# A two-level Strassen kernel in fp32: block 0's second load in two parts, weight loads held back, and six more products split a third time

## The chip, the core and the metric

The kernel runs on one core of one Trainium2 chip. The time is device microseconds of one execution. The engines named below are PE (TensorE, matrix products), DVE (VectorE), ACT (ScalarE), POOL (GpSimd, which here also issues the gathers) and SP (SyncE, which issues the other transfers).

## What is computed

The input x is 64 sequences of 64 tokens, 1024 features each, in fp32. Two steps are added to it:

```
x = x + A0[id0] . (B0[id0] . x)             # per sequence: an adapter of rank 16
base   = W x                                 # 1024 x 1024
logits = Wr x + 5 * onehot(id1)              # 8 experts, the best two get softmax weights
lora   = sum over experts of gate_e * B1_e (A1_e x)
x = x + base + 2 * lora
```

The kernel keeps tokens along the free axis, so x is 1024 x 4096 (features x tokens) and almost all the work is W x.

## The kernel before

The 4096 tokens are 8 blocks of 512. Two blocks make a pair, and there are four pairs, `s` = 0 to 3. For each block, `early` does the first adapter: `turn` transposes the gathered rows of B0 (tile `gb`) on PE into `pt`, ACT copies them to `bt`; `project` multiplies them with x into `pb`, DVE masks that into `bx`; `adapt` multiplies `bx` with the gathered rows of A0 (tile `ga`) into four `px` tiles for each half of the features, and DVE adds these to x. `late` does the router: `rows` gives `ph`, `gates` the expert weights on DVE, `weigh` transposes them through `pg` into `hg`.

`products` computes W x for a pair as 2 x 2 blocks with the Strassen-Winograd scheme, twice nested. The seven outer products have the numbers n in `ORDER = (1, 2, 6, 7, 5, 3, 4)`. Each of them has seven inner products k of a 256 x 256 weight tile (`s` tiles, 256 KB) with 256 x 256 tokens: four fp32 matmuls of 128 x 128 weights on 256 columns, in PSUM tiles `pa` and `pb`. Pair 0 makes the sums of weights that the scheme needs and writes them to `s_kept` in DRAM; later pairs load them. Inner products of some n can be split a third time ("fine"): seven matmuls on 128 columns in place of four on 256, in a tile `pf`, in four parts that the order puts between other products. A fine product needs sums of weights (`sf`, four operations of POOL or DVE, kept in DRAM as `f_kept` and loaded later), sums of tokens (`tt`, three operations), three ACT copies into `cp`, and two DVE additions of 128 x 256. `fine_of(s, n)` says which k are split: none in pair 0, k = 2 and 4 in the later pairs, only k = 2 in the last product of the last pair.

Nothing is ordered by hand. Every step is handed to a `Plan` with the engines that can do it and its estimated cost, what it reads and writes, the slot it takes, and a due time `at`. `Plan.order` (L64) simulates the engines with these estimates and fixes each engine's instruction order; the program then waits on semaphores only. `behind` makes a step be issued only after another one has been issued. A `hold` is a POOL copy of one column into a tile that is about to be loaded: the load has to wait for it, and it waits for the data that it reads. In the kernel before:

- `load(0, 0)` loads the first half of block 0 (features 0 to 511) in two transfers of 512 KB; `load(0, 1)` loads the second half in one of 1 MB, held until the first of these two has landed.
- `load_w` loads the sixteen 256 KB tiles of W, each behind the load of A1 (`a_sb`), which is itself held until block 0's `gb` has landed.
- `b1_sb` is loaded behind A1.
- PSUM slots are eight: four of tag `l` (`pt`, `pb` of `project`, `px`, `ph`, `pg`, part of `pf`), two `a`, two `b`.
- In `products`, pairs with `s < FINE` take one branch for the order of the steps (L1222 to L1232), the others the branch for fine products.

Of the kernel before, what the change touches and what calls it, by code (L numbers as in the profile page):

```python
# [14 lines left out]
P = 128  # L15
# [159 lines left out]
def kernel(  # L175
# [52 lines left out]
    TB = 512  # L228
    NBLK = NT // TB
    NSUP = NBLK // 2  # L230
# [16 lines left out]
    WHOLE = {(0, 1)}  # L247

    FINE = 1
    FOURTH = (1, 2, 6, 7, 5, 3, 4)  # L250
    THIRD = ()

    pe, dve = Pinned(tc, nc.tensor), Pinned(tc, nc.vector)
    act, pool, sp = Pinned(tc, nc.scalar), Pinned(tc, nc.gpsimd), Pinned(tc, nc.sync)
# [14 lines left out]
    def new(tag, shape, name):  # L269
        return pools[tag].tile(shape, F32, tag=tag, name=name)  # L270
# [38 lines left out]
    def consts():  # L309
        plan.add({"SP": 0.4}, lambda e: sp.dma_start(wr_c, wr), [], [("wr_c",)], -53, kb=8)  # L310
        plan.add(
            {"SP": 0.4}, lambda e: sp.dma_start(ids1_sb, ids1[0:1, :].to_broadcast([P, NB])),
            [], [("ids1",)], -53, kb=32,
        )

        def hold(e):

            pool.tensor_copy(a1_sb[:, 0, :1], made["gb", 0][:, :1])

        plan.add({"POOL": 0.2}, hold, [(("gb", 0),)], [("a1",)], -56)  # L320
        plan.add({"SP": 0.4}, lambda e: sp.dma_start(a1_sb[:, :, :P], a1), [], [("a1",)], -45, kb=512)
        plan.add({"SP": 0.4}, lambda e: sp.dma_start(b1_sb, b1), [], [("b1",)], -29, kb=512, behind=[("a1",)])

        def spread(e):
            pool.tensor_copy(a1_sb[:, :, P:], wr_c)

        plan.add({"POOL": 0.3}, spread, [("wr_c",)], [("wr",)], -45)
# [26 lines left out]
    def part(t, cs=range(HC), gs=range(NG)):  # L354
        return [(t, c, g) for c in cs for g in gs]
# [7 lines left out]
    def load(k, i, at):  # L363
        t = ("x", k, i)

        held = (k, i) == (0, 1)

        def hold(e):

            made[t] = new("q", [P, HC, TB], f"x_{k}_{i}")  # L370
            pool.tensor_copy(made[t][:, 0, :1], made["x", 0, 0][:, 0, :1])


        cuts = ((0, HC // 2), (HC // 2, HC)) if (k, i) == (0, 0) else ((0, HC),)

        def fn(c0, c1):
            if not held and c0 == 0:
                made[t] = new("q", [P, HC, TB], f"x_{k}_{i}")
            sp.dma_start(
                made[t][:, c0:c1],  # L380
                xT[(i * HC + c0) * P : (i * HC + c1) * P, k * TB : (k + 1) * TB].rearrange(
                    "(c p) t -> p c t", p=P
                ),
            )

        if held:
            plan.add(
                {"POOL": 0.2}, hold, part(("x", 0, 0), [0]), part(t), at, [("q", t)]
            )
        for c0, c1 in cuts:  # L390
            plan.add(
                {"SP": 0.5}, lambda e, c0=c0, c1=c1: fn(c0, c1),
                [], part(t, range(c0, c1)), at, [("q", t)] * (not held and c0 == 0),
                kb=256 * (c1 - c0), behind=[("a1",)] * (k == 1) + [(t, 0, 0)] * (c0 > 0),
            )
# [249 lines left out]

    def load_w(i, j, at):
        t = w_name[i, j]

        def fn(e):
            made[t] = new("s", [P, QC, QO], f"w_{i}{j}")  # L650
            sp.dma_start(made[t], w[:, j * QC : (j + 1) * QC, i * QO : (i + 1) * QO])

        plan.add({"SP": 0.4}, fn, [], [(t,)], at, [("s", t)], kb=256, behind=[("a1",)])

    def add_identity(i, at):

# [18 lines left out]
    def fine_of(s, n):  # L675

        if s < FINE:
            return ()
        if (s, n) == (NSUP - 1, ORDER[-1]):
            return (2,)  # L680
        return (2,) + (4,) * (n in FOURTH) + (3,) * (n in THIRD)


    def combine(out, a, b, op, at, engines):
# [33 lines left out]
    def weights(s, n, at):  # L718

        out = {}  # L720
        if s > 0:
            for i, m in enumerate(ORDER):
                out[m] = t = ("s", s, n, m)

                def fn(e, t=t, m=m):
                    made[t] = new("s", [P, QC, QO], f"s_{s}_{n}{m}")
                    sp.dma_start(made[t].rearrange("p c o -> p (c o)"), s_kept[n - 1, m - 1])

                plan.add({"SP": 0.1}, fn, [("kept", n, m)], [(t,)], at + i - 8, [("s", t)], kb=256)
            wt[n] = out  # L730
            for k in fine_of(s, n):
                fine_weights(s, n, k, out[k], at + (k == 4) * 5)
            return
        m = m_q[n]
        out = {1: m[0, 0], 2: m[0, 1], 4: m[1, 1]}
        for k, (u, v, op) in {
            5: ((1, 0), (1, 1), ALU.add),
            6: (5, (0, 0), ALU.subtract),
            7: ((0, 0), (1, 0), ALU.subtract),
            3: ((0, 1), 6, ALU.subtract),  # L740
        }.items():
            out[k] = ("s", s, n, k)
            uu = m[u] if isinstance(u, tuple) else out[u]
            vv = m[v] if isinstance(v, tuple) else out[v]
            combine(out[k], uu, vv, op, at - 4, {"DVE": 0.65})
        for k in ORDER:
            t = out[k]

            def keep(e, t=t, k=k):
                sp.dma_start(s_kept[n - 1, k - 1], made[t].rearrange("p c o -> p (c o)"))  # L750

            plan.add({"SP": 0.1}, keep, [(t,)], [("kept", n, k)], at + 4, kb=256)
        wt[n] = out

    def fine_weights(s, n, k, a, at):

        t, kept = ("sf", s, n, k), f_kept[n - 1, k - 2]

        def blocks():
            made[t] = new("s", [P, QC, QO], f"sf_{s}_{n}{k}")  # L760
            return grid(made[t])

        def grid(m):
            return m.rearrange("p c (o w) -> p (c o) w", w=P)

        def load(e):
            blocks()
            sp.dma_start(made[t].rearrange("p c o -> p (c o)"), kept)

        def sums(x):  # L770
            def fn(e):
                f, w4 = blocks() if x == 0 else grid(made[t]), grid(made[a])
                a11, a21, a12, a22 = (w4[:, y] for y in range(4))
                v = engine[e]
                if x == 0:
                    v.tensor_tensor(f[:, 0], a21, a22, ALU.add)
                elif x == 1:
                    v.tensor_tensor(f[:, 1], f[:, 0], a11, ALU.subtract)
                elif x == 2:
                    v.tensor_tensor(f[:, 2], a11, a21, ALU.subtract)  # L780
                else:
                    v.tensor_tensor(f[:, 3], a12, f[:, 1], ALU.subtract)

            return fn

        def keep(e):
            sp.dma_start(kept, made[t].rearrange("p c o -> p (c o)"))

        if s == FINE:
            for x in range(4):  # L790
                plan.add(
                    {"DVE": 0.29, "POOL": 0.48}, sums(x), [(a,)] + [(t, y) for y in range(x)], [(t, x)], at - 3,
                    [("s", t)] * (x == 0), sb=True,
                )
            plan.add({"SP": 0.1}, keep, [(t, x) for x in range(4)], [("fine", n, k)], at + 4, kb=256)
        else:
            plan.add({"SP": 0.1}, load, [("fine", n, k)], [(t, x) for x in range(4)], at - 6, [("s", t)], kb=256)
        wt[n]["fine", k] = t
# [83 lines left out]
    def products(s):  # L882
# [328 lines left out]
        for n in ORDER:  # L1211
            after = ORDER[ORDER.index(n) + 1] if n != ORDER[-1] else None
            if (s, n) in WHOLE:
# [5 lines left out]
                    if x == 1 and after is not None:  # L1219
                        begin(after)  # L1220
                continue
            if s < FINE:  # L1222
                step(n, 1)
                if rest:
                    step(*rest[0])
                step(n, 2)
                if rest:
                    step(*rest[1])
                if after is not None:
                    begin(after)  # L1230
                for k in (6, 7, 5):
                    step(n, k)  # L1232
            else:

                step(n, 1)
                going.append([n, 2, 0])
                advance()
                for k in rest:
                    step(*k)
                    advance()  # L1240
                if after is not None:
                    begin(after)

                for k in (6, 7, 5):
                    step(n, k)
                    if k in (6, 5) and k - 2 in fine_of(s, n):
                        going.append([n, k - 2, 0])
                    advance()
                rest = [(n, k) for k in (3, 4) if k not in fine_of(s, n)]
                if last(n):  # L1250
                    rest = [(n, 4), (n, 3)]
                continue
# [14 lines left out]
    for q0, at in (((0, 0), -43), ((0, 2), -39), ((2, 0), -37), ((2, 2), -36)):  # L1267
        for i, j in ((0, 0), (0, 1), (1, 0), (1, 1)):

            load_w(q0[0] + i, q0[1] + j, at + 2 * i * (at == -43))  # L1270
    early(0, -40)
    biases()
    for i in range(4):
# [74 lines left out]
```

## Time and profile before

| | |
|---|---|
| median of 3 runs | 515.52 us (515.12 to 516.07) |
| the profiled execution, its own time | 514.86 us |
| its span, first to last instruction | 513.0 us, so 1.9 us lie around it |
| PE busy | 499.8 us, 97% of the span |
| DVE busy | 410.3 us, 80% |
| POOL, ACT busy | 105.4 us (21%), 75.8 us (15%) |
| moved by DMA | 110.00 MB, mean 214 GB/s |

In the profile a matmul of fp32 on 128 or 256 columns shows as two records, so an inner product of four matmuls is `x8`. A chain line reads: start in us, length in us, engine, tile, number of records. The busy time of a PE group is the union of overlapping records; the chain's lengths are the pace at which they follow one another.

### The profile page before, as it was taken

To read this page: it belongs to the slowest core of one execution; us is meant where nothing else is said; L and a number is where in the kernel's file an instruction comes from. 1 tells how busy PE (TensorE), PEld (TensorE's weight loads), DVE (VectorE), ACT (ScalarE), POOL (GpSimd) and SP (SyncE) were. 2 spreads that over 40 slices of the span, in tenths; PEclk is the share of its full clock that TensorE was granted. 3 is DMA by queue.
4 is the path that set the end of the run, shared out by engine and by line. 5 is a ranking of instruction groups with operands and counts; after the bars stand their busy time and mean duration, and the time that the engine had idled before them with its cause. 6 is when DMAs were issued, how large, how long until landed. Compare 5 with 4: busy or idle time off the path is not lost.

```text
span 513.0 us, 9559 instructions
## 1 busy us (share of the span) xinstructions
PE 499.8 (97%) x3678; PEld 442.5 (86%) x3678; DVE 410.3 (80%) x822; ACT 75.8 (15%) x204; POOL 105.4 (21%) x175
## 2 busy tenths in 40 slices
PE   3999999999999999999999999999999999999997
PEld 2857888889888998889888998889989999999996
DVE  0788899989878777888989789874889988875964
ACT  1111100001000211111201221102301112112210
POOL 3002000020432433442233021201212120212100
PEclk9999999999999999999999999999999999999999
DMA  8999273964895648875567645972756665673023
GB/s 286 374 369 351 83 270 120 332 247 141 300 312 201 208 130 284 309 247 187 185 226 236 221 131 173 356 260 81 240 173 205 231 202 142 228 192 96 0 115 132
DMA packets 60172, 110.00 MB, mean 214 GB/s; under 512 B 5600, under 2 KB 11744, under 8 KB 60128
## 3 DMA queue, kind: packets, MB, share of 16 engines
q1 hardware_dynamic: 57824, 101.01, 58.7%
q0 software_dynamic: 2304, 8.39, 4.9%
q8 instruction: 29, 0.48, 0.4%
q14 instruction: 15, 0.12, 0.1%
HBM read 76.09 MB, written 33.29 MB: 213 GB/s over the span
## 4 chain that ended last, share of the span: by engine, by line
PE 94%; DMA 4%; DVE 1%; issue 0%; SPq 0%
PE pa L29 38%; PE pb L29 19%; PE pf L29 16%; PE ph L29 12%; PE px L29 3%; PE pw L29 3%; DMA x<-in_xT 3%; PE pt L29 2%; DMA gb<-in_b,idx 1%; PE pg L29 1%; DVE s L29 0%; DMA ids_sb<-in_ids 0%; DVE ti L29 0%; DVE u L29 0%; DVE x L29 0%
## 5 line engine op out<-in xcount | busy, mean ns | idle before, releaser
L29 PE MATMUL pa<-ti,s 128*128 128x256 f32 x432 | 102.1, 380 | 0.0
L29 PEld LDWEIGHTS pa<-ti,s 128*128 128x128 f32 x432 | 78.7, 190 | 9.3
L29 ACT COPY cp<-pf 128x128 f32<-128x128 f32 (+1 forms) x123 | 37.0, 302 | 214.4 <-PE pf L29 201.3
L29 PEld LDWEIGHTS ph<-a_sb,x 128*128 128x128 f32 x512 | 61.7, 190 | 1.5 <-issue 0.9
L29 PE MATMUL ph<-a_sb,x 128*128 128x136 f32 x512 | 62.5, 279 | 0.2 <-issue 0.2
L29 PE MATMUL pb<-ti,s 128*128 128x256 f32 x224 | 55.8, 380 | 0.0
L29 PE MATMUL pa<-x,s 128*128 128x256 f32 x216 | 52.7, 381 | 0.0
L29 PE MATMUL pf<-tt,sf 128*128 128x128 f32 x246 | 47.5, 277 | 0.0
L29 DVE TENSOR_TENSOR x<-px,x 128x512 f32<-128x512 f32 x64 | 39.9, 683 | 6.8 <-PE px L29 6.8
L29 PEld LDWEIGHTS pb<-ti,s 128*128 128x128 f32 x224 | 40.9, 190 | 4.8 <-issue 0.2
L29 PEld LDWEIGHTS pf<-tt,sf 128*128 128x128 f32 x246 | 41.4, 191 | 3.8 <-issue 0.4
L29 PEld LDWEIGHTS pa<-x,s 128*128 128x128 f32 x216 | 39.3, 190 | 5.0 <-issue 0.4
L29 PE MATMUL pa<-t,s 128*128 128x256 f32 x168 | 41.2, 380 | 0.0
L29 PEld LDWEIGHTS pa<-t,s 128*128 128x128 f32 x168 | 30.8, 190 | 3.9 <-issue 0.2
L29 POOL TENSOR_TENSOR tt<-ti 128x256 f32<-128x256 f32 x16 | 12.3, 771 | 93.5 <-PE pf L29 60.2
L29 DVE TENSOR_TENSOR o<-pa,u 128x512 f32<-128x512 f32 x32 | 22.0, 687 | 9.9 <-PE pa L29 9.6
L29 POOL TENSOR_TENSOR tt<-x 128x256 f32<-128x256 f32 x11 | 9.2, 833 | 93.9 <-PE pf L29 47.7
L29 DVE TENSOR_TENSOR o<-pb,o 128x512 f32<-128x512 f32 x35 | 23.1, 687 | 2.7 <-PE pb L29 1.9
L29 DVE TENSOR_TENSOR ti<-t 128x512 f32<-128x512 f32 x24 | 16.7, 696 | 8.4 <-PE pb L29 6.4
L29 DVE TENSOR_TENSOR ti<-x,ti 128x512 f32<-128x512 f32 x30 | 21.7, 724 | 1.2 <-PE pb L29 0.6
L29 DVE TENSOR_TENSOR o<-o,cp 128x256 f32<-128x256 f32 x46 | 19.6, 425 | 2.5
L29 POOL TENSOR_TENSOR sf<-s 128x128 f32<-128x128 f32 x27 | 14.0, 518 | 35.8 <-DMA s<-s_kept 14.5
(154 smaller groups left out, 807.6 us busy)
## 6 DMA issues: line engine op xcount, KB each, us to landing
s<-s_kept SPq DMA_DIRECT2D x147, 256.0 KB
x<-in_xT SPq DMA_DIRECT2D x15, 1024.0 KB
out_T<-o SPq DMA_DIRECT2D x30, 512.0 KB
s_kept<-s SPq DMA_DIRECT2D x28, 256.0 KB
sf<-f_kept SPq DMA_DIRECT2D x27, 256.0 KB
s_kept<-w SPq DMA_DIRECT2D x18, 256.0 KB
w<-in_w SPq DMA_DIRECT2D x16, 256.0 KB
f_kept<-sf SPq DMA_DIRECT2D x14, 256.0 KB
```

What stands on the lines that cost most here:

```text
L29: return self._tc.keep_in_program_order(f(*args, **kwargs))
```

## The change

Six edits:

1. `load(0, 1)` is two transfers of 512 KB. The first is held until the first transfer of `load(0, 0)` has landed, the second until the second has.
2. The load of W tile (1, 0) is held (by a POOL copy) until the first half of block 1 has landed, and all W tiles but (0, 0), (0, 1) and (1, 0) come behind it.
3. `b1_sb` is loaded behind W tile (1, 0).
4. `THIRD = (3, 4)`: in pairs 1 and 2 the outer products 3 and 4 split k = 3 as well, four fine products in all.
5. `EARLY = {(0, 3), (0, 4)}`: in pair 0 the outer products 3 and 4 split k = 2, two fine products. Their `sf` are made and kept in pair 0 and loaded in pair 1.
6. In pair 0 the products 3 and 4 take the order of steps of the fine branch.

The planner sees other transfers and costs, and so it also orders other steps anew. On PE the order is the same up to the router of block 3 but for one place: for block 0, before it was `px_0`, `px_1`, then both transposes `pt` of block 1, then `ph`; now it is the first transpose of block 1, `px_1`, `px_0`, half of `ph`, the second transpose, the other half. DVE adds `px` to x in the order half 1, half 1, half 0 where it was half 0, half 0, half 1.

```diff
+    EARLY = {(0, 3), (0, 4)}
     FOURTH = (1, 2, 6, 7, 5, 3, 4)
-    THIRD = ()
+    THIRD = (3, 4)
...
-        cuts = ((0, HC // 2), (HC // 2, HC)) if (k, i) == (0, 0) else ((0, HC),)
+        half = HC // 2
+        def hold(c0, by):
+            def fn(e):
+                if c0 == 0:
+                    made[t] = new("q", [P, HC, TB], f"x_{k}_{i}")
+                pool.tensor_copy(made[t][:, c0, :1], made["x", 0, 0][:, by, :1])
+            return fn
+        cuts = ((0, half), (half, HC)) if k == 0 else ((0, HC),)
...
-                {"POOL": 0.2}, hold, part(("x", 0, 0), [0]), part(t), at, [("q", t)]
+                {"POOL": 0.2}, hold(0, 0), part(("x", 0, 0), [0]), part(t, range(half)), at, [("q", t)]
+            )
+            plan.add(
+                {"POOL": 0.2}, hold(half, half), part(("x", 0, 0), [half]), part(t, range(half, HC)), at
             )
...
+        held = (i, j) == (1, 0)
+        def hold(e):
+            made[t] = new("s", [P, QC, QO], f"w_{i}{j}")
+            pool.tensor_copy(made[t][:, 0, :1], made["x", 1, 0][:, 0, :1])
+        if held:
+            plan.add({"POOL": 0.2}, hold, part(("x", 1, 0), [0]), [(t,)], at, [("s", t)])
...
-        plan.add({"SP": 0.4}, fn, [], [(t,)], at, [("s", t)], kb=256, behind=[("a1",)])
+        plan.add(
+            {"SP": 0.4}, fn, [], [(t,)], at, [("s", t)] * (not held), kb=256,
+            behind=[("a1",)] + [(w_name[1, 0],)] * ((i, j) not in ((0, 0), (0, 1), (1, 0))),
+        )
...
         if s < FINE:
-            return ()
+            return (2,) * ((s, n) in EARLY)
...
-        return (2,) + (4,) * (n in FOURTH) + (3,) * (n in THIRD)
+        return (2,) + (4,) * (n in FOURTH) + (3,) * (n in THIRD and s < NSUP - 1)
...
         wt[n] = out
+        for k in fine_of(s, n):
+            fine_weights(s, n, k, out[k], at)
...
-        if s == FINE:
+        if not any(k in fine_of(x, n) for x in range(s)):
...
-            if s < FINE:
+            if not fine_of(s, n):
                 step(n, 1)
...
+    plan.add(
+        {"SP": 0.4}, lambda e: sp.dma_start(b1_sb, b1), [], [("b1",)], -29, kb=512, behind=[(w_name[1, 0],)]
+    )
```

More of the change, by code (lines that the diff above doesn't have):

```diff
@@ L321, in consts @@
         plan.add({"SP": 0.4}, lambda e: sp.dma_start(a1_sb[:, :, :P], a1), [], [("a1",)], -45, kb=512)
-        plan.add({"SP": 0.4}, lambda e: sp.dma_start(b1_sb, b1), [], [("b1",)], -29, kb=512, behind=[("a1",)])
         def spread(e):
@@ L366, in load @@
         held = (k, i) == (0, 1)
-        def hold(e):
-            made[t] = new("q", [P, HC, TB], f"x_{k}_{i}")
-            pool.tensor_copy(made[t][:, 0, :1], made["x", 0, 0][:, 0, :1])
-        cuts = ((0, HC // 2), (HC // 2, HC)) if (k, i) == (0, 0) else ((0, HC),)
+        half = HC // 2
[6 more added lines that the diff above has]
+        cuts = ((0, half), (half, HC)) if k == 0 else ((0, HC),)
         def fn(c0, c1):
@@ L647, in load_w @@
         t = w_name[i, j]
+        held = (i, j) == (1, 0)
[4 more added lines that the diff above has]
+            plan.add({"POOL": 0.2}, hold, part(("x", 1, 0), [0]), [(t,)], at, [("s", t)])
         def fn(e):
-            made[t] = new("s", [P, QC, QO], f"w_{i}{j}")
+            if not held:
+                made[t] = new("s", [P, QC, QO], f"w_{i}{j}")
             sp.dma_start(made[t], w[:, j * QC : (j + 1) * QC, i * QO : (i + 1) * QO])
-        plan.add({"SP": 0.4}, fn, [], [(t,)], at, [("s", t)], kb=256, behind=[("a1",)])
+        plan.add(
+            {"SP": 0.4}, fn, [], [(t,)], at, [("s", t)] * (not held), kb=256,
+            behind=[("a1",)] + [(w_name[1, 0],)] * ((i, j) not in ((0, 0), (0, 1), (1, 0))),
+        )
     def add_identity(i, at):
```

## The prediction

> **What bounds the kernel now.** I read the page first, then the chain of waits stage by stage, then the landing times of the gathers.
>
> ```profile
> PE 499.8 (97%) x3678; PEld 442.5 (86%) x3678; DVE 410.3 (80%) x822; ACT 75.8 (15%) x204; POOL 105.4 (21%) x175
> PE 94%; DMA 4%; DVE 1%; issue 0%; SPq 0%
> L29 PE MATMUL pb<-x,bt 128*32 128x128 f32 x512 | 17.9, 291 | 0.4 <-DMA x<-in_xT 0.3
> ```
>
> PE is the bound. Of the 513.0 us it is idle for 13.2: 8.8 before its first instruction, 3.3 behind its last, and 1.1 in between. The third line has the largest stall after the start, 0.3 us, where block 2's tokens land (at 99.4 us). So nearly every us of PE work added or removed, and every stall in the start, goes into the end one for one; nothing later has idle time to absorb it.
>
> The chain from 0 to 30 us shows the start:
>
> ```profile
> 3.08 5.59 DMA gb<-in_b,idx
> 8.80 1.94 PE pt L29 x8
> 10.74 3.39 PE pb L29 x64
> 14.15 0.30 DVE bx L29
> 14.50 2.07 PE px L29 x64
> 16.56 1.18 PE pt L29 x8
> 17.93 7.65 PE ph L29 x64
> 25.59 1.89 PE pb L29 x64
> ```
>
> PE starts when the gather of block 0 lands. `px` waits for `bx`. Block 1's transposes (`pt` at 16.56) lie behind both `px` groups. DVE is the partner:
>
> ```profile
> 15.74 4.88 DVE L29 TENSOR_TENSOR x<-px,x 128x512 f32<-128x512 f32 x8 [1.30 <-PE px L29]
> ```
>
> It begins 1.24 us after the first `px` and adds one tile every 0.61 us. Then the gather of block 1, on POOL's timeline, and its landing, from the tile view of `gb` narrowed to that issue; below, the same row for all eight gathers of `gb`:
>
> ```profile
> 9.04 0.97 POOL L29 DMA_INDIRECT gb<-in_b,idx  x1
> DMA to landing us min/median/max: 6.6/6.6/6.6
> ...
> DMA to landing us min/median/max: 4.3/6.1/8.1
> ```
>
> It is issued at 9.04 and lands at 9.04 + 6.6 = 15.6 us. Before, nobody needs it until 16.5.
>
> **The change: the start.** The new PE order puts the first transpose of block 1 ahead of both `px`, which had been free to run at 14.50. PE runs in order, so `px`, then DVE's additions, then `ph` queue behind a gather that lands at 15.6. Step by step: the transpose takes half of 1.18, or 0.5 with its start; `px` starts at 15.64 + 0.5 = 16.1 in place of 14.50 (+1.6). `ph` needs the first tile of both halves. DVE now does half 1 twice before half 0, so this is its third addition: 1.24 + 2 x 0.61 + 0.68 = 3.2 us after `px` starts, at 19.3; before it was 17.93, and DVE's third addition (end 17.6) was not what it waited for. Then `ph`, 7.65 or a little less as DVE is further ahead, and inside it the second transpose, 0.45: block 1's `pb` starts at 27.3 in place of 25.59. **Cost +1.7 us.**
>
> The landing is what decides. It keeps its row only if the gather meets the same traffic, and it does so nearly: it is issued on the landing of block 0's gather, as before, and behind it SP still sends A1, two W tiles and 2 MB of block 1. Bounds: with the quickest of the eight, 4.3, it lands at 13.3, ahead of `bx`; `px` then starts at about 14.6 and only the second transpose inside `ph` is left, +0.2. With the slowest, 8.1, it lands at 17.1: +3.2. The 6.6 is the same gather in the same place, so I take it. [...]
>
> Splitting the load of half 1 adds one SP transfer and one POOL copy. The copy stands behind the issue of `ga` (5.40 to 6.37), so the second part is issued at about 6.7 and not at 5.27. Its first reader is the last quarter of `pb`, at 13.2; before, nothing waited for this load in `pb`. It may let the `ga` gather in earlier, and with it block 1's `gb`; this is the gain that I leave out of the sum (down to the +0.2). It does not touch 8.80, since block 0's gather is issued at 3.08, ahead of all of it.
>
> Holding the W tiles costs nothing that PE sees. Tile (1, 0) is issued when block 1's first half lands, with the 1 MB of the second half still to come to keep the queue filled, and its reader runs at 36.3. One store of W tile (0, 1) now stands in SP's queue before it and waits for that tile's landing, which is older than block 1's. `b1_sb` is first read after 54 us. POOL's copy for W stands behind the `ga` gather of block 1 and before that of block 2 (41.2), whose row shows it waiting anyway.
>
> **The change: six fine products.** From the chain between 254 and 286 us:
>
> ```profile
> 261.16 1.73 PE pa L29 x8
> 264.84 2.20 PE pf L29 x16
> 271.58 1.11 PE pf L29 x10
> 282.86 1.98 PE pf L29 x14
> ```
>
> An inner product is 1.73 us. A narrow `pf` record is 1.11 / 10 = 0.111 (the difference of the other two, 0.22 for two, agrees), so a fine product of 14 is 1.55 and saves 0.18. Fine products come in four parts, and each seam can show a weight load: some `pa` x8 stand in the chain with 1.92 in place of 1.73. I take 0.03 us for each as the mean over all seams, since most rows have 1.73. Saved: 6 x (0.18 - 0.03) = **-0.9 us** (bounds -1.1 with no seam, -0.5 with one more exposed load of 0.19 in every second product and more).
>
> What they add elsewhere: two DVE additions each (mean 425 ns), and for k = 3 one more eviction (0.69), as `pa` is emptied after k = 5 already: 6 x 0.85 + 4 x 0.69 = 7.9 us of DVE; 18 ACT copies of 0.3; token sums of three POOL operations (0.77, 0.5, 0.6) and weight sums of four for k = 3, the ones for `EARLY` only move from pair 1 to pair 0. ACT and POOL have 80% idle; the weight sums for the early products stand behind gathers at 112 and 122 and take 2.6 us, 6 us or more before PE wants them. On SP: four `f_kept` transfers for k = 3, and two loads in pair 1 where sums were made; with 59% of the engines' time taken there is room. DVE is the one to look at:
>
> ```profile
> 255.00:290.00 35.00, 35.00 (x224) 31.50 (x223) 30.22 (x51) 5.06 (x15) 8.56 (x13) 1.00 0.70 231
> ```
>
> The third number after the length is DVE's 30.2 of 35 us, where products 3 and 4 of a pair run. With 3.1 more it is at 95%. [...] Below, more ACT and POOL help could also remove seams. I bound this by -0.3 and +1.5 and take **+0.3**.
>
> Sum: +1.7 - 0.9 + 0.3 = +1.1 us. The profiled execution, 513.0 of span and 1.9 around it, is 514.86, within 0.7 us of the median; its sum is 516.0, and laid on the median of 515.52 it is **516.6 us**. About 0.2% (1.03 us) is what a measurement of this kernel can tell from no change; the sum is just over it.
>
> **The rivals.**
>
> *A. The gather lands in time.* The place is block 1's first transpose, the point 14.1 us: a `gb` that lands by then costs PE nothing. For it: the later second part of the load, and the fastest row, 4.3. Against: A1 and 2 MB for block 1 are in the queue. The start is then +0.2 and the sum 0.2 - 0.9 + 0.0 = -0.7: 514.8, and with the seams kept low -1.1: 514.4. This is the case that ends faster; chance 0.25, of which 0.2 go past the bound.
>
> *B. DVE or the W loads become the bound in products 3 and 4.* For it: 95% in that stretch, two more `s` slots in use, so loads come later. Against: PE has no stall there now, and the loads lie 10 us and more ahead. Four stalls of 0.5 to 0.7 us on top of the start: +3.5, 519.0; chance 0.13.
>
> *C. The stall cools PE.* The row for it: `pb` took 3.39 us at the start and 1.89 for the same 64 records later, so PE runs at about half pace for its first 5 us. [...] The new gap is 14.1 to 15.6, or 1.5. [...] No gap of this length is in the trace. Chance 0.05.
>
> [...]
>
> **How the numbers follow.** My forecast, the gather at its old row, has 0.45: 516.6, with its own range 515.9 to 518.0, longer upward since the bounds of the DVE term are. A has 0.25, D 0.12, B 0.13, C 0.05. Slower by over 0.2%, above 516.55: all of B and C and six tenths of the forecast, 0.45. Faster by over 0.2%, below 514.5: 0.2, out of A. The rest, 0.35, is within the bound. The range from 514.2 to 518.2 takes in A, D and the forecast; what is left out is B, C and the ends.
>
> **What would show it.** Right: block 1's first `pt` in the chain behind DMA `gb`, idle time of PE of about 1.5 us before it, `px` at 16, `ph` at 19.3; `pf` groups with 84 records more and PE busy lower by about 0.9. Wrong: `px` at 14.6 (A); idle before PE in the pairs' products 3 and 4 released by DVE or by `s` loads (B); `ph` with more than 8.5 us (C); a first `pt` much before or after 8.80, which I have not foreseen.

## The result, and the profile after

The change makes the kernel slower. The median is 520.07 us (518.64 to 520.77, six runs) against 515.47 us (514.89 to 516.07, six runs) of the kernel before beside it: ratio 1.0074, 95% interval 1.0058 to 1.0089. The forecast was 516.6 with a range that ended at 518.2. The profiled execution of the changed kernel took 518.64 us (span 516.9), the quickest of its six; before it was 514.86 (span 513.0).

From the page after, the rows of busy time, of the chain by engine, and of two groups that the prediction spoke of. (This group of `pf` had x246 before. Over all groups of `pf` on 128 columns the trace has 658 records and 574 before, the 84 more that were predicted.)

```profile
PE 500.5 (97%) x3714; PEld 444.0 (86%) x3714; DVE 420.9 (81%) x837; ACT 81.2 (16%) x222; POOL 121.5 (24%) x204
PE 93%; DMA 4%; DVE 1%; issue 0%; SPq 0%; POOL 0%
L29 PE MATMUL pf<-tt,sf 128*128 128x128 f32 x282 | 54.0, 278 | 0.0
...
L29 PE MATMUL pb<-x,bt 128*32 128x128 f32 x512 | 17.9, 291 | 0.8 <-DMA x<-in_xT 0.8
```

PE's busy time should have gone down by 0.9 us and it went up by 0.7. More products are split, so something else on PE takes longer: `px` alone went from 18.5 to 20.0 us. The chain of the first 32 us (start, length, what) shows it:

```profile
2.93 6.09 DMA gb<-in_b,idx
...
9.40 7.20 DMA gb<-in_b,idx
16.59 0.04 issue
16.64 0.66 PE pt L29 x4
17.30 3.54 PE px L29 x64
20.84 0.80 issue
21.63 3.95 PE ph L29 x32
25.58 0.44 PE pt L29 x4
26.02 3.71 PE ph L29 x32
29.73 1.88 PE pb L29 x64
```

Block 1's `pb` starts at 29.73; before, at 25.59. That is 4.14 us, more than the whole difference between the ends of PE's work (3.79: 509.65 and 513.44, by the last matmul record in each trace). Two things are to be seen. The transpose `pt` waits for the second `gb`, as predicted, though it lands later than predicted; PE's timeline has 2.20 us of idle time before it:

```profile
16.64 0.66 PE L29 MATMUL pt<-ident,gb 128*128 128x128 f32 x4 [2.20 <-DMA gb<-in_b,idx]
```

And `px`, 64 records as before, takes 3.54 us where it took 2.07. The stretches of the trace cut at the steps of the granted clock (as the trace records it, in shares of full speed) suggest why; the experiment e5 tests it. The columns are the length, busy time of PE, PEld, DVE, ACT and POOL with their records, then the granted clock, the DMA share and GB/s:

```profile
14.07:17.49 3.42, 1.22 (x24) 0.78 (x20) 0.29 (x1) 0.09 (x1) 0.00 (x0) 1.00 1.03 353
17.49:20.90 3.41, 3.35 (x64) 3.05 (x60) 1.35 (x3) 0.49 (x1) 0.00 (x0) 0.50 1.06 393
20.90:24.31 3.41, 2.68 (x23) 2.71 (x24) 3.41 (x6) 0.00 (x0) 1.14 (x2) 1.00 0.89 283
```

In one stretch of 3.41 us PE worked only 1.22 us, and for the next 3.41 us its clock was 0.50. Before, the clock stayed at 1.00 from 13.7 us, its first record, to the end of the work.

The mean granted clock is on record for every execution. One stretch of 3.41 us at 0.50 lowers it by 0.0033, and a step to 0.50 after PE's last work by 0.0009 (before) and 0.0010 (after). So, as an estimate from their means, the six executions of the changed kernel lost the clock for one stretch (0.996, 0.997, 0.997), two (0.993, 0.992) or three (0.989), and none kept it. The profiled one is a short case: by it the change costs 3.8 us, by the medians 4.6.

POOL's row of the gather and its landing, and DVE's additions that follow `px`:

```profile
9.40 0.97 POOL L29 DMA_INDIRECT gb<-in_b,idx  x1
DMA to landing us min/median/max: 7.2/7.2/7.2
...
19.19 1.29 DVE L29 TENSOR_TENSOR x<-px,x 128x512 f32<-128x512 f32 x2 [4.38 <-PE px L29]
20.84 3.68 DVE L29 TENSOR_TENSOR x<-px,x 128x512 f32<-128x512 f32 x6 [0.36 <-PE px L29]
```

DVE has its first additions at 19.19 instead of 15.74 and pauses behind `px`. The third of them starts at 20.84, and `ph` follows it, as the prediction had it.

### The profile page after: what moved, and what is told of

It reads as the page before. It is cut to its first block, busy times and chain, and to the rows that moved or that the text cites. A ratio compares the mean times of both kernels' runs of the same rounds, so it can differ in the third digit from the quotient of the medians.

```text
span 516.9 us, 9731 instructions
## 1 busy us (share of the span) xinstructions
PE 500.5 (97%) x3714; PEld 444.0 (86%) x3714; DVE 420.9 (81%) x837; ACT 81.2 (16%) x222; POOL 121.5 (24%) x204
## 4 chain that ended last, share of the span: by engine, by line
PE 93%; DMA 4%; DVE 1%; issue 0%; SPq 0%; POOL 0%
PE pa L29 36%; PE pf L29 20%; PE pb L29 18%; PE ph L29 12%; PE px L29 4%; PE pw L29 3%; DMA gb<-in_b,idx 3%; DMA x<-in_xT 1%; PE pt L29 1%; PE pg L29 1%; DVE s L29 0%; DMA ids_sb<-in_ids 0%; DVE ti L29 0%; DVE u L29 0%; DVE x L29 0%
## 5 line engine op out<-in xcount | busy, mean ns | idle before, releaser
L29 ACT COPY cp<-pf 128x256 f32<-128x256 f32 (+1 forms) x141 | 42.1, 302 | 207.5 <-PE pf L29 207.2
L29 PE MATMUL pf<-tt,sf 128*128 128x128 f32 x282 | 54.0, 278 | 0.0
L29 PEld LDWEIGHTS pf<-tt,sf 128*128 128x128 f32 x282 | 46.8, 191 | 4.5 <-issue 0.8
L29 PE MATMUL pa<-x,s 128*128 128x256 f32 x200 | 48.6, 381 | 0.0
L29 PEld LDWEIGHTS pa<-x,s 128*128 128x128 f32 x200 | 36.3, 190 | 4.5 <-issue 0.4
L29 PE MATMUL pa<-t,s 128*128 128x256 f32 x152 | 36.9, 379 | 0.0
L29 PEld LDWEIGHTS pa<-t,s 128*128 128x128 f32 x152 | 27.8, 190 | 3.1
L29 POOL TENSOR_TENSOR tt<-t 128x256 f32<-128x256 f32 x11 | 9.0, 814 | 87.2 <-PE pf L29 53.2
L29 DVE TENSOR_TENSOR o<-o,cp 128x256 f32<-128x256 f32 x58 | 25.9, 449 | 3.3
L29 DVE TENSOR_TENSOR o<-pf,o 128x512 f32<-128x512 f32 x29 | 19.9, 686 | 4.6 <-PE pf L29 4.4
```

The costliest lines, as they stand in the source:

```text
L29: return self._tc.keep_in_program_order(f(*args, **kwargs))
```

## The experiments

Two theories stood against each other. *The start:* all of the loss comes from one place in PE's order, block 1's first transpose ahead of both `px`; part of it is the wait for the gather, part the clock that falls after the wait. *The loads or the products:* the new loads are late by themselves, or the six fine products bring waits of their own in the pairs. Fillers below are transposes of the identity into a `pt` tile that is written anew right after; they compute nothing that the kernel needs. Each ratio is to the kernel before on the same chip; the chip is not the same for all experiments.

**Only the loads (e1).** The changed kernel without its fine products:

```diff
-    EARLY = {(0, 3), (0, 4)}
+    EARLY = set()
...
-    THIRD = (3, 4)
+    THIRD = ()
```

> Only the load edits (block 0's second half in two parts, W held, b1 behind W), no fine products added. Theory 1 (the PE order that comes with the load edits puts block 1's transpose ahead of px; PE then waits for a gather, and that idle time brings the clock down): block 1's pb starts 4.1 us later than before, so about 519.4 to 520.2 against 515.5, slower than the whole change by the 0.4 to 0.8 us that the fine products save. Theory 2 (the fine products are what costs): no more than 1 us slower than before.

Measured: 518.44 us (516.57 to 519.89) against 515.62, ratio 1.0049 (1.0032 to 1.0066). A loss is there without a single new product, and so is PE's order of the start. It was expected to be the larger one, and it is smaller than that of the whole change (1.0074), though the intervals overlap. The clocks on record go with it: of six executions three kept the clock (1.000; 516.57, 517.93 and 518.36 us), two lost it for one stretch (518.52 and 518.82) and one for two (519.89). The last is the profiled one:

```profile
14.66:18.08 3.42, 1.74 (x44) 1.48 (x44) 0.29 (x1) 0.58 (x1) 0.00 (x0) 1.00 1.05 371
18.08:21.49 3.41, 2.62 (x40) 2.35 (x36) 2.88 (x5) 0.00 (x0) 0.94 (x1) 0.50 1.05 385
21.49:24.90 3.41, 3.41 (x16) 3.41 (x16) 3.33 (x10) 0.00 (x0) 0.18 (x1) 0.50 0.98 337
24.90:28.32 3.42, 3.42 (x31) 3.42 (x31) 3.13 (x7) 0.97 (x2) 0.00 (x0) 1.00 0.95 310
```

The first stretch at 0.50 had 2.62 us of work (77%) and was followed by a second at 0.50; that one was full of work, 3.41 us, and was followed by 1.00.

**Only the fine products (e2).** The changed kernel with the loads of the kernel before (cuts, holds and `b1_sb` as they were); the planner then gives the old order of the start.

```diff
+        plan.add({"SP": 0.4}, lambda e: sp.dma_start(b1_sb, b1), [], [("b1",)], -29, kb=512, behind=[("a1",)])
...
-        cuts = ((0, half), (half, HC)) if k == 0 else ((0, HC),)
+        cuts = ((0, HC // 2), (HC // 2, HC)) if (k, i) == (0, 0) else ((0, HC),)
...
-        held = (i, j) == (1, 0)
...
```

> Only the six fine products, the loads and PE's order in the start as before. Theory 1: faster than before by 0.4 to 0.9 us (0.1 to 0.2%), px at 14.5 and ph at 17.9 us as before. Theory 2: slower than before by 3 us or more.

Measured: 514.99 us, ratio 0.9995 (0.9984 to 1.0006). No loss, and no gain clear of the noise, where 0.4 to 0.9 us were expected. In the profiled execution 0.88 us are seen to go at 144 us, in pair 0, from the chain and PE's timeline:

```profile
135.35 7.72 DMA out_T<-o
...
143.17 0.70 DVE o L29
...
143.91 1.99 PE pa L29 x8
...
143.91 1.99 PE L29 MATMUL pa<-ti,s 128*128 128x256 f32 x8 [0.88 <-DVE o L29]
```

A store of an output tile takes 7.72 us where the page's median for `out_T` stores is 3.1; DVE wants to write that tile again, and PE waits 0.88 us for the accumulator that DVE has not emptied.

**The changed kernel, one order undone (e3).** Everything of the change stays; block 1's transposes are issued behind both `px` of block 0:

```diff
             [("l", pt)] + [("bt", bt)] * (g == 0),
+            behind=[(("px", 0, h, 0),) for h in range(2)] * (k == 1),
```

> The whole change, but block 1's transposes are put behind both px of block 0, and with that PE's and DVE's order in the start is that of before; the loads stay changed. Theory 1: the 4 us go, 515.0 to 515.8 (0.8 less for the fine products, some tenths more for the gather of block 0 that landed at 9.02). Rival of theory 1 (the split and held loads make everything in the start later, whatever the order): 518 or more.

Measured: 514.78 us, ratio 0.9985 (0.9971 to 1.0000). The loss is gone, with all of the new loads and products in place. The chain of the start is that of the kernel before again, 0.65 us later:

```profile
15.15 2.07 PE px L29 x64
17.21 1.18 PE pt L29 x8
...
18.59 7.65 PE ph L29 x64
26.24 1.88 PE pb L29 x64
```

**The kernel before, that order alone (e4).** Nothing of the change but its order of the start: the first transpose of block 1 ahead of both `px`, and with that the second one inside `ph`:

```diff
-            list(zip(tags, px)),
+            list(zip(tags, px)), behind=[(("pt", 1, 0),)] * (k == 0),
...
-    early(0, -40)
+    turn(0, 0, -40)
+    turn(0, 1, -40)
+    turn(1, 0, -12)
+    project(0, -38)
+    adapt(0, 0, -37)
+    adapt(0, 1, -36)
...
-    early(1, -12)
+    turn(1, 1, -12)
...
```

> The kernel before, with nothing changed but that block 1's first transpose is put ahead of block 0's px (and px, ph and the second transpose in the order of the changed kernel). Theory 1: 3 to 4.5 us slower than before, PE idle for 1.5 to 2.2 us at 14 to 16.6 us, the granted clock at 0.5 for part of px. Rival (the loads): within 1 us of before.

Measured: 519.08 us (516.75 to 522.32), ratio 1.0080 (1.0050 to 1.0110). That order alone reproduces the whole loss:

```profile
9.39 6.58 DMA gb<-in_b,idx
16.01 1.08 PE pt L29 x4
17.09 3.16 PE px L29 x64
...
16.01 1.08 PE L29 MATMUL pt<-ident,gb 128*128 128x128 f32 x4 [1.78 <-DMA gb<-in_b,idx]
...
12.68:16.09 3.41, 1.36 (x41) 0.92 (x34) 0.29 (x1) 0.00 (x0) 0.00 (x0) 1.00 1.02 346
16.09:19.50 3.41, 3.41 (x48) 3.08 (x52) 0.31 (x1) 0.59 (x1) 0.00 (x0) 0.50 1.05 386
```

Here the gather keeps the latency of before, 6.58 us, and `px` is slow all the same: PE is idle for 1.78 us before the transpose, and the clock falls at 16.09, just after the transpose has begun. By their means, one of the six executions kept the clock (516.75 us), three lost it for one stretch (518.13 to 519.18) and two for three (521.01 and 522.32). With so few the order of the times is a hint only, as a longer wait could bring both the fall and the time.

**The wait filled (e5).** The changed kernel with 20 fillers in PE's wait. They take away the idle time but not the wait, so this splits the loss in two.

```diff
+            if (k, g) == (1, 0):
+                for c in range(20):
+                    pe.transpose(made[pt][:, c % PER, :], ident, ident)
             for c in range(PER):
```

> The whole change, and in PE's wait for block 1's gather 20 transposes of the identity, written to the tile that the real transpose then overwrites, so that PE is busy from 14.4 to 16.6 us. Theory 1 (the second half of the loss is the clock, lowered because PE stood idle): the granted clock stays at 1.00, px takes 2.1 us in place of 3.5, block 1's pb starts 1.7 to 2.2 us earlier, so about 518.0 against 520.1; the other half, the wait, stays. Rival (px is slow for another reason, its PSUM slots or the transfers beside it): no change, 519.5 to 520.5.

Measured: 517.78 us, ratio 1.0044 (1.0030 to 1.0058), against 1.0074 without the fillers. The clock stays up (in 21 of the 22 executions, by their means) and `px` is back at its old pace, while the gather is waited for as before:

```profile
9.76 7.05 DMA gb<-in_b,idx
...
16.86 0.66 PE pt L29 x4
17.51 2.00 PE px L29 x64
19.51 1.17 issue
20.68 3.94 PE ph L29 x32
...
12.34:15.76 3.42, 3.26 (x67) 2.83 (x60) 0.29 (x1) 0.00 (x0) 0.00 (x0) 1.00 1.05 348
15.76:19.17 3.41, 3.03 (x71) 2.63 (x73) 0.48 (x1) 0.59 (x1) 0.00 (x0) 1.00 1.06 379
```

By the ratios the clock is 0.0030 x 515.5 = 1.5 us of the loss and the wait the other 2.3 us. The two intervals just touch, and they come from different occasions, so the profiles have to carry it as well: from the start of `px` to that of `ph` it is 4.33 us in the changed kernel and 3.17 us here (the prediction had 3.2), so 1.2 us for one stretch at half clock.

**Warm from the beginning (e6).** The kernel of e3 with 48 fillers ahead of the first `pt`, to see whether the slow first `pb` can be won back:

```diff
+            if (k, g) == (0, 0):
+                for c in range(48):
+                    pe.transpose(made[pt][:, c % PER, :], ident, ident)
```

> The change with block 1's transposes behind px (as in the run before with that order), and 48 transposes of the identity ahead of block 0's first one, from about 1.5 us to 8.5 us, while PE would wait for the first gather. Theory 1 (only PE's idle time sets the clock): pt and pb of block 0 run at full pace, about 1 us for the 8 and 2 us for the 64 records, px waits for ga at 12.2 to 12.7 in place of 14.5, then the transposes of block 1 wait for their gather at 15.6 to 16.5, and ph starts about 1 us sooner: 513.5 to 514.0 against 514.8 without. Rival (the fillers bring PE nothing since the gathers bound the start anyway): 514.6 to 515.2.

Measured: 515.5 us against 515.74, ratio 0.9988 (0.9973 to 1.0002): no better than e3, where a gain was expected. `pb` now runs faster (its first 48 records take 1.52 us; in the kernel before all 64 took 3.39), and so it arrives too early and waits for x. In the profiled execution (517.37 us, the slowest of 22) the clock falls after that new idle time; only one other execution has as low a mean clock, so the fall is not why the median gains nothing; the wait for x may be:

```profile
13.13 0.65 PE L29 MATMUL pb<-x,bt 128*32 128x128 f32 x16 [1.66 <-DMA x<-in_xT]
...
11.31:14.73 3.42, 1.36 (x41) 0.96 (x37) 0.29 (x1) 0.00 (x0) 0.00 (x0) 1.00 1.07 362
14.73:18.14 3.41, 3.41 (x59) 3.19 (x52) 1.91 (x4) 0.00 (x0) 0.26 (x1) 0.50 1.07 369
```

**Warm, with the order and loads of before (e7, e8).** The 48 fillers and 10 more ahead of block 1's first `pt`, in the kernel before (e7) and in the kernel of e2 (e8):

```diff
+            if (k, g) == (0, 0):
+                for c in range(48):
+                    pe.transpose(made[pt][:, c % PER, :], ident, ident)
+            if (k, g) == (1, 0):
+                for c in range(10):
+                    pe.transpose(made[pt][:, c % PER, :], ident, ident)
```

> The kernel before with its own order of PE (both px, then block 1's transposes), with 48 transposes of the identity ahead of the first transpose of block 0 and 10 ahead of the first transpose of block 1. They compute nothing that is needed; they only keep PE from standing still. It measures the price of the clock by itself, in a kernel without any other part of the change. Theory 'half of the loss is the clock, and PE's idle time sets it': block 0's pt and pb run at full pace (1.94 + 3.39 become about 1.1 + 1.5), px starts when the second half of x (about 11.8) has passed pb, at about 12.9 in place of 14.50; the granted clock stays at 1.0 through 25 us; the time is 1.0 to 1.6 us shorter than before, ratio 0.997 to 0.998. Rival 'the granted clock in the records is only a by-product, the slow matmuls of the start come from weights or data that arrive late': pb still takes about 3.4 us with PE busy ahead of it, and the ratio is 1.000.

> The six fine products with the loads and the order of the start of the kernel before, and the same 48 and 10 transposes of the identity as in the run with the kernel before (they compute nothing that is needed). Theory: gains of the warm start (1.0 to 1.6 us) and of the fine products (0.0 to 0.8 us, measured as 0.9995 by themselves) add, ratio 0.995 to 0.9975. Rival 'what is won in the start is lost again at the first store of product 5 in pair 0, where DVE waits for the store': PE's stall at about 144 us is over 1.5 us and the ratio is 0.998 or more.

Measured: e7 517.38 us against 516.27, ratio 1.0028 (1.0014 to 1.0042); e8 517.62 us, ratio 1.0033 (1.0017 to 1.0048). Both theories of e7 are wrong in what they expected of the time. The matmuls did become faster (the last 32 of `pb` take 1.11 us, and 1.28 in e9 without fillers), which weights or data that arrive late do not explain; but little was won, as x's second half landed at 13.87 us and PE waited 1.67 us for it:

```profile
4.76 9.11 DMA x<-in_xT
...
14.01 1.11 PE pb L29 x32
...
15.49 1.25 PE px L29 x31
...
20.08 7.65 PE ph L29 x64
27.73 1.89 PE pb L29 x64
...
14.01 1.08 PE L29 MATMUL pb<-x,bt 128*32 128x128 f32 x32 [1.67 <-DMA x<-in_xT]
```

The kernel e9, on the same chip with a cold start, has that landing at the same 13.87, its `px` at 15.66 and its block 1 `pb` at 26.75, a microsecond sooner. So the warm start won 0.17 us up to `px`. From there to block 1's `pb` e7 takes 12.24 us and e9 11.09. The 1.15 us between them are what the ten fillers take on PE's timeline, from 17.49 to 18.64, ahead of a transpose whose gather was in at 17.17. (The last thing that `ph` waited for is then an addition of DVE that ended at 19.83; whether it would hold `ph` without the fillers is not shown.) The clock may have a part as well: four of e7's ten executions have a mean of 0.993 to 0.997 and take 518.2 to 519.2 us, the other six 516.4 to 517.5. e8's rival is right on the ratio and wrong on its place: the stall at 144.88 us is 0.46 us, and the start has e7's 12.24 us.

**Only the four third products (e9, e10).** The kernel of e2 without the two early products, cold (e9) and with the fillers of e7 (e10):

```diff
-    EARLY = {(0, 3), (0, 4)}
+    EARLY = set()
```

> Only the four third fine products (k = 3 of the outer products 3 and 4 in pairs 1 and 2); the loads, the start and pair 0 are those of the kernel before. Theory 'a fine product saves 0.15 us and more of PE everywhere, but the two early ones in pair 0 move the first store of product 5 to a later place in SP's queue and PE pays for it at about 144 us': this kernel has no stall of PE at 143 to 146 us and is 0.6 us shorter than before, ratio 0.9985 to 0.9990; with that it beats the kernel with all six (0.9995). Rival 'a fine product saves next to nothing, its seams eat it': ratio 0.9995 to 1.0005, PE's busy time lower by less than 0.3 us.

> The four third fine products as in the run with them alone, and the 48 and 10 transposes of the identity (they compute nothing that is needed). If the gains add, this is the fastest of the kernels here: 1.0 to 1.6 us from the start and 0.5 us from the products, ratio 0.9955 to 0.997. If what is won in the start is given back at block 2's tokens or at the first store of product 5 in pair 0, a stall of PE over 1 us shows there and the ratio is 0.998 or more.

Measured: e9 516.27 us against 516.27, ratio 1.0001 (0.9986 to 1.0017); e10 516.64 us, ratio 1.0019 (1.0005 to 1.0033). The expected gain of e9 (0.9985 to 0.9990) does not show, and neither does a loss: the ratio is where its rival had it, with an interval of 0.8 us on both sides that reaches the gain. PE's busy time speaks against the rival (499.0 us, and 499.8 before). The stall at 144 us is absent, as expected. e10 was expected to be the fastest and is not; it carries the cost of the fillers like e7.

What a single time cannot resolve, the profiles can in part, if PE's stalls are taken out. PE's busy time from the start of block 1's `pb` to PE's last record is 483.7 us in each of the four kernels without new products (before, e1, e4, e7); in those with all six (after, e2, e3, e5, e6, e8) it is 483.0, 483.2, 482.8, 483.4, 483.1 and 483.2, in those with four (e9, e10) 483.1 and 483.1. So the six save about 0.6 us of PE's time, and the four alone about as much, which is some 0.15 us for each of the four. What the two early ones save is not shown: 0.3 us was expected of them, and the kernels with six differ by 0.6 among themselves. A stall at 144 to 145 us is found in e2 (0.88), e6 (2.23) and e8 (0.46), all with the early products, and in no kernel without them; three others with them (after, e3, e5) have none either. The output store issued ahead of it, at 134 to 139 us, takes 6.4 to 9.1 us in all six.

## Why the prediction was wrong

**The step of the start: the mechanism held.** The chain has block 1's first `pt` behind DMA `gb`, PE is idle before it, and `px`, DVE and `ph` queue behind that. e4 and e3 show that this one order is sufficient and necessary for the loss. Of the 4.14 us by which block 1's `pb` is later, 0.36 come from block 0's gather, which landed at 9.02 and not 8.66; six other kernels with the loads of before had it at 8.98 (e2) to 9.88 us (e7), so I don't put it down to the change. 0.60 are the second gather: 7.20 us and not 6.6. That was inside the bounds of the landing, on the slow side. The five kernels with the new loads had 6.9 to 7.4 us, the seven with the old ones 6.4 to 7.2; whether the new loads have a part in it stays open. 1.2 are the clock (from e5). What is left, 2.0, is the term that was predicted as +1.7: the transpose takes 0.7 where 0.5 was put, and `ph` with the second transpose 8.1 where 8.0 was.

**The step that failed is rival C, "The stall cools PE", and with it the sum, which has no term for the clock.** I saw the mechanism, gave it 0.05, and left it out of the sum: that a gap of 1.5 us takes nothing from the clock was my estimate, and no trace of before shows it. That C ends above the range was an estimate as well; the measured median, 520.07 us, lies there. The traces with the clock down show this: each lowered clock between two of full clock lasted one stretch of 3.41 us (after, e4) or two in a row (e1), and the stretch ahead of the fall had 1.22 us of PE's work (after), 1.36 (e4 and e6) or 1.74 (e1, 51% as the cut stretch shows it). With the measured numbers the sum would have been 1.7 + 0.6 + 0.4 + 1.2 in the start and about -0.3 behind it, +3.6 us; the profiled execution has +3.8. The medians have +4.6, and by their mean clocks half of the six executions lost it for more than the one stretch of this sum.

In the changed kernel the clock was down for one stretch and cost 1.2 us. In e1 it was down for two, with `ph` x32 at 6.00 us: from `px` to block 1's `pb` it takes 13.75 us there and 11.26 in e5, which kept the clock, so 2.5 us. My sign of it, `ph` with more than 8.5 us, was a poor one: here the stretch at 0.50 fell on `px` (3.54 us), and `ph` with its transpose took 8.1. That the changed kernel's runs are spread over 2.1 us fits a clock that is down for one stretch or more: by the mean clocks one, two and three. It does not explain every run, as 520.77 us came with one alone, and the mean does not say where in a run the clock fell.

**The fine products: right in kind, too high in size.** The term was -0.9; PE's time shows about -0.6. The four third products save some 0.15 us each, as predicted; for the two early ones the profiles are too far apart to tell.

**The DVE term of +0.3.** No run shows this term. Idle time of PE between the start and the end is 0.76 us after and 0.40 before: +0.36, but at another place, where block 2's tokens land (0.76 at 104.2, before 0.31 at 99.4). DVE is not behind it, and e1, e3, e4 and e5 have no such wait, so that the size came near the term is luck. DVE's work grew by 10.6 us, more than the 7.9 of the prediction. With the early products DVE can be late at 144 us (e2, e6, e8), released by an output store, which I had not named.

**Rival A** (the gather in time) fell with `px` at 17.30. **Rival B** (DVE the bound in products 3 and 4) fell as well. The stretch that answers to the one shown of before, moved by the 4 us:

```profile
259.00:294.00 35.00, 35.00 (x238) 31.88 (x238) 32.19 (x56) 7.33 (x22) 9.78 (x15) 1.00 0.75 247
```

PE is busy for all of the 35 us; DVE has 32.2 (92%), 2.0 more than before, not the 3.1 that I added, and no wait of PE comes with it. **Rival D** has 0.12 among the chances, for a gather that comes a little sooner; no run shows what that would take off the start. In the changed kernel the gather took 7.2 us from its issue, 0.6 more than before, so D fell too; no gather of block 1 in any kernel took less than 6.3.

No kernel here beats the one before beyond doubt. The nearest is e3, the change with its one order undone, at 0.9985 with an interval that ends at 1.0000; by the two ratios it is 0.9% below the changed kernel.

## What to carry to other kernels

When a step moves ahead on an in-order engine, price the wait and then ask what the idle engine does to its clock: here a wait of 2.20 us was followed by a stretch at 0.50 that cost another 1.2. Do not excuse a gap because it is short: a wait of 1.66 us was followed by such a stretch in e6, one of 1.67 us in e7 was not. Look at the share of work around the gap, and take the case that it falls badly into the range. And before filling or warming anything, look at what lands next: with a warm start PE only waited longer for a load (1.66 us in e6, 1.67 in e7), and fillers that outlast the wait are a cost of their own (1.15 us in e7).

## What the runs showed that was not expected

The length of the gap did not tell by itself whether the clock falls: a wait of 1.66 us was followed by a fall in e6, one of 1.67 us in e7 was not. Nor did the share of PE's work in the 3.41 us ahead in every case. Stretches with 36% to 40% (1.22 us after, 1.36 in e4 and e6) were followed by one at 0.50; after one with 66% (e5, 2.24 of 3.41 us from 19.17) the clock stayed. With 1.74 us of 3.42 (51%) both are on record: e1 fell, e7 stayed up:

```profile
8.04:11.45 3.41, 1.73 (x21) 1.26 (x22) 0.00 (x0) 0.83 (x2) 1.15 (x2) 1.00 1.03 409
11.45:14.86 3.41, 1.74 (x64) 1.46 (x56) 0.00 (x0) 0.24 (x1) 0.00 (x0) 1.00 0.98 336
14.86:18.28 3.42, 3.02 (x81) 2.67 (x72) 1.83 (x4) 0.00 (x0) 0.34 (x1) 1.00 1.07 372
```

Of the stretches at 0.50, the one with 77% (2.62 us, e1) was followed by another at 0.50, those with 98% (3.35 us, after) and 100% (3.41 us, e4 and the second of e1) by 1.00. In e7 no step marks where a stretch begins, so its shares depend on where the trace is cut. What sets the fall is not shown by so few cases. That the work is counted in busy time, and not in records or columns, is my reading; no run separates these.
